# The last of a unit's seven softmax additions as an accumulating DMA from GpSimd

## The chip, the cores and the metric

The kernel runs on one core of a Trainium2 chip. The time is device microseconds of one execution. A core has five engines with queues of their own, each worked off in order: TensorE (PE; its weight loads are shown as PEld), VectorE (DVE), ScalarE (ACT), GpSimd (POOL) and SyncE (SP), which issues DMAs. Sixteen DMA engines carry the transfers. Engines wait for each other through semaphores.

## What is computed

The input is x of shape (4, 1024, 128), in fp32. Three layers follow each other: x + 0.5 FFN(layernorm(x)), then x + attention(layernorm(x)), then x + 0.5 FFN(layernorm(x)) again. The FFN is a mixture of 8 experts with routing weights. What matters here is the attention, of 16 heads of 64 in each of the 4 batches:

```
c_q, c_kv = h @ w_down_q.T, h @ w_down_kv.T
q, k, v   = up-projections of c_q, c_kv, split in heads; q and k are rotated
scores    = q @ k.T / 8                      # (4, 16, 1024, 1024)
attn      = softmax(scores)
out       = (attn @ v) @ w_out.T + residual
```

## The kernel before

**Units.** The attention is cut into 64 units. A unit is two heads (one pair P) and 512 queries; a pair has two units, an even one and an odd one. The keys come in 8 slots of 128. The probabilities stand transposed, with the keys on the partitions: a slot gives a tile p of 128 keys x (2 heads x 512 queries), 128x1024 fp32 or 512 KB.

**A unit's work.** First the scores: `score` (L921) multiplies K and Q in parts on TensorE for each slot and head and subtracts the row maxima by a fourth matmul (L933); ACT takes the exponential into p (L937). When both heads of a slot are there, `accumulate` (L941) is called. Between the scores stand the matmuls for the maxima of later slots (`passA`, L907), which DVE reduces (L908); they run 15 slots ahead. The maxima go through DRAM into one row (`max_row`, L915). At the unit's end come the denominators of the unit before (`den`), then the value matmuls (`values`, L957: the latent keys ckn times p) and ACT's copy of them (L960).

**The sums.** The softmax denominator of a query is a sum over all keys, thus over 8 slots and 128 partitions. POOL adds tiles: at slot 1 it adds p of slots 0 and 1 into acc, at each later slot it adds that slot's p to acc (L949). Seven additions give one tile acc. `den` (L962) then sums over the partitions on TensorE: a matmul with ones against acc, in four parts of 256 columns (L969; each shows as two passes, eight in all). `direct(U)` says how many of the unit's last tiles POOL leaves out: those are multiplied by ones on TensorE as well, in the same sum. Before the change it is 1 for every third unit up to 53 (U = 2, 5, ..., 53: 18 units), 3 for the last unit and 0 for the others.

**After the sums.** ACT copies the denominators to dsb (L971), SP writes them to DRAM (d<-dsb, L975) and reads them back in another order (dT<-d, L977) one unit later. DVE takes the reciprocal (rT<-dT, L988). Output matmuls with the matrix G (L992), ACT's scaling by rT (L1008) and DVE's addition to X (L1002) finish the unit. rT stands in DVE's queue between the reductions of the maxima, after the unit's scores.

**What else runs beside it.** Each unit also prepares a piece of the rotated q and k of a later pair (`rope`: matmuls L797, DVE L810 to L816, ACT L824, POOL's subtraction `lo` L832). SP writes the results to DRAM (qs, ks, 512 KB each) and loads them as QT and KT in 16 transfers of 128 KB per pair; these loads are issued in the even units. SP also fetches C_l for the next piece. The order of all this is written out by hand in `run`, with places within a unit ("mid", "end", "side", "scale").

**Buffers.** p has 10 buffers, so slot s writes into the buffer of slot s - 10. acc has 2. SP issues all DMAs of the kernel; POOL issues none.

Of the kernel before, what the change touches and what calls it, by code (L numbers as in the profile page):

```python
# [13 lines left out]
ALU = mybir.AluOpType  # L14
# [16 lines left out]
NUNIT = NSLOT // 8  # L31
# [10 lines left out]

def direct(U):

    return 3 if U == NUNIT - 1 else 1 if U % 3 == 2 and U < 56 else 0


class Kernel:
# [892 lines left out]
    def accumulate(self, s):  # L941

        nc = self.nc
        U, c = divmod(s, 8)
        if c == 0:
            self.acc_of[U] = self.accp.tile([128, 2, 512], F32, name="acc")
        elif c < 8 - direct(U):
            acc = self.acc_of[U]
            nc.gpsimd.tensor_tensor(acc, self.p_of[s - 1] if c == 1 else acc, self.p_of[s], ALU.add)  # L949
# [12 lines left out]
    def den(self, U):  # L962

        nc = self.nc
        pd = self.psS[3]
        parts = [self.p_of[8 * U + c] for c in range(8 - direct(U), 8)] + [self.acc_of[U]]
        for k, part in enumerate(parts):
            for n in range(4):
                nc.tensor.matmul(pd[32 * n:32 * n + 32, 0:256], self.ones, part[:, n // 2, 256 * (n % 2):256 * (n % 2) + 256], start=k == 0, stop=k == len(parts) - 1)  # L969
        dsb = self.op1.tile([128, 256], F32, name="dsb")  # L970
        nc.scalar.copy(dsb, pd[:, 0:256])  # L971
        dT = self.ms.tile([128, 8], F32, name="dT")

        d1 = self.dram.tile([4, 256], F32, name=f"d1_{U % 4}")
        nc.sync.dma_start(out=d1, in_=dsb[0:128:32, :])  # L975
        g = 2 * U + 4
        self.at(g + (U == NUNIT - 1), lambda: nc.sync.dma_start(out=dT, in_=d1.rearrange("(h x) (y p) -> p (h x y)", x=2, p=128)), "mid")  # L977
        self.at(g + (2 if U == NUNIT - 1 else 1), lambda: self.outp(U, self.osb_of.pop(U), dT), "side")
# [325 lines left out]
```

## Time and profile before

| | |
|---|---|
| median of 3 runs | 1623.9 us (1623.08 to 1624.63) |
| the profiled execution | 1627.57 us, of which span 1625.8 us |
| granted TensorE clock in it | 0.994 |
| attention stage | about 225 to 1465 us of the span |
| TensorE busy | 97% of the span |
| POOL busy | 90% |
| DVE, ACT busy | 76%, 68% |
| DMA engines busy, mean | 50.5% (212.27 MB moved) |

The page gives busy times by engine, a picture of the span in 40 slices, the chain of work that ended last and the costliest groups of instructions by source line. In a group's line stand the line, the engine and operation, the tiles written and read with their shapes, the count, then the busy time in us with the mean of one in ns, and the idle time of the engine before these instructions with what ended it. The chain of work that ended last is TensorE for 83% of the span; its largest pieces are the value matmuls (L957, 28%) and the scores (L933, 20%). POOL is in it with 5%, and 3% are the denominators (L969).

Other views of the same trace are used below: the timeline of one engine in a window, the busy time by engine in several windows, a source line with those that wait for it, and the list of waits. The trace also holds every count of the semaphores, from which the landing of a DMA is read.

### The profile page before, as it was taken

How to read it: one execution, taken by the hardware profiler on the slowest of the kernel's cores; microseconds unless marked ns; L12 is line 12 of the kernel's file. 1: busy time of each engine (PE TensorE's matmuls, PEld its weight loads, DVE VectorE, ACT ScalarE, POOL GpSimd, SP SyncE). 2: the span in 40 equal slices, each digit the busy share in tenths (PEclk: the TensorE clock that was granted, in tenths of full speed). 3: DMA queues.
4: the chain of work that ended last, by engine and by line, in shares of the span. 5: the costliest groups of instructions: out<-in, count | busy, mean ns of one | idle time of the engine just before them, and what ended most of it. 6: DMA issues, size and time to landing. Idle time of an engine off the chain costs nothing.

```text
span 1625.8 us, 31310 instructions
## 1 busy us (share of the span) xinstructions
PE 1575.9 (97%) x11068; PEld 1049.8 (65%) x11068; DVE 1242.0 (76%) x2198; ACT 1109.7 (68%) x2488; POOL 1464.3 (90%) x857
## 2 busy tenths in 40 slices
PE   7998999999999999999999999999999999998998
PEld 6876766566666666666666666666665666556776
DVE  6556678788888888888888887888787866616897
ACT  4676557768777667877776777776677676665554
POOL 4668889999999999999999999999999999994676
PEclk9999999999999999999999999999999999999999
DMA  7024565555555556555555566555556542025543
GB/s 226 5 60 148 169 161 133 136 152 137 144 131 138 137 147 154 144 144 131 144 131 144 132 151 159 139 151 132 143 142 156 125 105 54 2 93 145 141 131 103
DMA packets 241149, 212.27 MB, mean 131 GB/s; under 512 B 157665, under 2 KB 170593, under 8 KB 240225
## 3 DMA queue, kind: packets, MB, share of 16 engines
q1 hardware_dynamic: 240992, 210.28, 50.1%
q8 instruction: 87, 1.43, 0.4%
q14 instruction: 70, 0.57, 0.1%
HBM read 130.39 MB, written 79.82 MB: 129 GB/s over the span
## 4 chain that ended last, share of the span: by engine, by line
PE 83%; POOL 5%; DVE 4%; ACT 3%; DMA 2%; issue 2%; SPq 1%; POOLq 0%; DVEq 0%; ACTq 0%
PE psc L957 28%; PE ps_s L933 20%; PE ps_a L907 7%; PE psx L933 4%; PE psc L933 3%; PE ps_s L463 3%; PE ps_s L969 3%; PE ps_s L543 3%; PE ps_s L797 2%; PE ps_s L992 2%; PE psx L498 2%; DVE m L908 2%; DMA dT<-d 1%; POOL X L447 1%; PE psc L434 1%
## 5 line engine op out<-in xcount | busy, mean ns | idle before, releaser
L949 POOL TENSOR_TENSOR acc<-acc,p 128x1024 f32<-128x1024 f32 x363 | 864.9, 2383 | 28.4
L908 DVE TENSOR_REDUCE m<-ps_a 128x1 f32<-128x512 f32 x1024 | 674.0, 686 | 205.9 <-PE ps_a L907 175.3
L937 ACT ACTIVATE p<-ps_s 128x512 f32<-128x512 f32 x768 | 411.5, 601 | 67.3 <-PE ps_s L933 50.9
L957 PE MATMUL psc<-p,ckn 128*64 128x512 f32 x2048 | 453.6, 595 | 0.0
L933 PE MATMUL ps_s<-QT,KT 64*128 64x512 f32 x2304 | 413.2, 394 | 0.3 <-DVE C_a L718 0.3
L907 PE MATMUL ps_a<-KT,QT 64*128 64x512 f32 x1024 | 388.0, 410 | 8.9 <-DVE m L908 7.7
L957 PEld LDWEIGHTS psc<-p,ckn 128*64 128x64 f32 x2048 | 141.3, 137 | 282.1 <-issue 282.1
L933 PEld LDWEIGHTS ps_s<-QT,KT 64*128 64x128 f32 x2304 | 279.2, 184 | 61.8 <-issue 19.7
L907 PEld LDWEIGHTS ps_a<-KT,QT 64*128 64x128 f32 x1024 | 174.2, 184 | 43.8 <-DVE m L908 17.9
L960 ACT COPY osb<-psc 128x512 f32<-128x512 f32 x64 | 37.6, 587 | 230.8 <-PE psc L957 230.8
L933 PE MATMUL ps_s<-maxr,one_row 64*128 64x512 f32 x768 | 188.9, 392 | 0.0
L949 POOL TENSOR_TENSOR acc<-p 128x1024 f32<-128x1024 f32 x64 | 153.3, 2395 | 5.3 <-ACT p L937 5.3
L832 POOL TENSOR_TENSOR eo<-eo,hi_r 128x1024 fp32r<-128x1024 f32 x55 | 132.4, 2407 | 0.0
L933 PE MATMUL psx<-QT,KT 64*128 64x512 f32 x384 | 119.1, 390 | 0.0
L933 PE MATMUL psc<-QT,KT 64*128 64x512 f32 x384 | 109.2, 390 | 0.0
L933 PEld LDWEIGHTS ps_s<-maxr,one_row 64*128 64x128 f32 x768 | 99.8, 184 | 11.9
L551 POOL TENSOR_TENSOR p<-eo,p 128x512 fp32r<-128x512 f32 x42 | 62.7, 1499 | 42.3 <-ACT p L550 33.5
L1008 ACT ACTIVATE psx<-psx,rT 128x128 f32<-128x128 f32 x248 | 85.2, 344 | 20.6 <-ACT p L937 11.2
L447 POOL TENSOR_TENSOR X<-X,dtmp 128x512 f32<-128x512 f32 x54 | 69.3, 1282 | 33.1 <-ACT dtmp L446 32.0
L1008 ACT ACTIVATE ps_s<-ps_s,rT 128x128 f32<-128x128 f32 x248 | 84.3, 340 | 6.0
L824 ACT CAST hi_r<-eo 128x512 fp32r<-128x512 f32 x128 | 73.7, 626 | 18.9 <-POOL eo L819 14.1
L937 ACT ACTIVATE p<-psc 128x512 f32<-128x512 f32 x128 | 77.4, 605 | 7.8 <-PE ps_a L907 2.8
(267 smaller groups left out, 2680.9 us busy)
## 6 DMA issues: line engine op xcount, KB each, us to landing
C_l<-cs SPq DMA_DIRECT2D x128, 256.0 KB
QT<-qs SPq DMA_DIRECT2D x256, 128.0 KB
KT<-ks SPq DMA_DIRECT2D x256, 128.0 KB
qs<-hi_r SPq DMA_DIRECT2D x32, 512.0 KB
qs<-eo SPq DMA_DIRECT2D x32, 512.0 KB
ks<-hi_r SPq DMA_DIRECT2D x32, 512.0 KB
ks<-eo SPq DMA_DIRECT2D x32, 512.0 KB
rt<-wt SPq DMA_DIRECT2D x52, 256.0 KB
```

The source lines that it names most:

```text
L447: nc.gpsimd.tensor_tensor(X[:, t:t + 4, :], X[:, t:t + 4, :], tmp, ALU.add)
L463: nc.tensor.matmul(p, w[:, a, e, :], xs[:, c, :], start=k == 0, stop=k == 2)
L551: (nc.gpsimd if m < N - 1 else nc.vector).tensor_tensor(sh[:, 1, :], hp, self.f(sh[:, 0, :]), ALU.subtract)
L824: nc.scalar.copy(w["hi"][:, k, :], w["eo"][:, k, :])
L832: nc.gpsimd.tensor_tensor(w["eo"].bitcast(F32R), w["eo"], self.f(w["hi"]), ALU.subtract)
L907: nc.tensor.matmul(self.psA[hh], self.QT[P % 3][r, 0, q0:q0 + 128], self.KT[P % 3][r, 0, kk * 512:kk * 512 + 512], start=True, stop=True)
L908: nc.vector.tensor_reduce(m[0][:, hh, qb, kk:kk + 1], self.psA[hh], AX.X, ALU.max)
L933: nc.tensor.matmul(ps, w, x, start=k == 0, stop=k == 3)
L937: nc.scalar.activation(self.p_of[s][:, hh, :], ps, AF.Exp, scale=0.125)
L949: nc.gpsimd.tensor_tensor(acc, self.p_of[s - 1] if c == 1 else acc, self.p_of[s], ALU.add)
L957: nc.tensor.matmul(self.psC[64 * hh:64 * hh + 64, :], self.ckn[b % 2][:, c, :], self.p_of[s][:, hh, :], start=c == 0, stop=c == 7)
L1008: nc.scalar.activation(po[hh][:, c], po[hh][:, c], AF.Identity, scale=rT[:, 4 * hh + i:4 * hh + i + 1])
```

## The change

Two lines. `direct` now gives 3 for the last unit and 0 for every other, so that no other unit leaves a tile to TensorE. And in `accumulate` the last slot's addition is no instruction of POOL's arithmetic any more: POOL issues a DMA that adds p of slot 7 to acc in SBUF. The other six additions stay on POOL (one line further down: L949 is L951 in the changed kernel, L957 is L959, L969 is L971; the DMA is L948).

```diff
 def direct(U):
 
-    return 3 if U == NUNIT - 1 else 1 if U % 3 == 2 and U < 56 else 0
+    return 3 if U == NUNIT - 1 else 0
...
         U, c = divmod(s, 8)
         if c == 0:
             self.acc_of[U] = self.accp.tile([128, 2, 512], F32, name="acc")
+        elif c == 7 and not direct(U):
+            nc.gpsimd.dma_start(out=self.acc_of[U], in_=self.p_of[s], accum_op=ALU.add)
         elif c < 8 - direct(U):
             acc = self.acc_of[U]
             nc.gpsimd.tensor_tensor(acc, self.p_of[s - 1] if c == 1 else acc, self.p_of[s], ALU.add)
```

In the instruction order of the changed kernel the DMA stands on POOL where the seventh addition stood, behind the sixth; it waits for ACT (the last tile p) and for POOL's own sixth addition. The denominators on TensorE wait for its landing.

## The prediction

> **What bounds the kernel now.** I read the page first, its busy times and its groups. The columns of a group are line, engine, operation, tiles, count, then busy us and the mean of one in ns, then the idle time before it.
>
> ```profile
> PE 1575.9 (97%) x11068; PEld 1049.8 (65%) x11068; DVE 1242.0 (76%) x2198; ACT 1109.7 (68%) x2488; POOL 1464.3 (90%) x857
> ...
> L949 POOL TENSOR_TENSOR acc<-acc,p 128x1024 f32<-128x1024 f32 x363 | 864.9, 2383 | 28.4
> ...
> L949 POOL TENSOR_TENSOR acc<-p 128x1024 f32<-128x1024 f32 x64 | 153.3, 2395 | 5.3 <-ACT p L937 5.3
> ```
>
> TensorE and POOL both look full, so the question is which of them the other waits for. The windows of the attention stage settle it: from 300 to 1310 us TensorE is busy for 1004.4 of 1010 us and POOL for 981.5. The view of the line of POOL's additions says who waits for them.
>
> ```profile
> who waited for it (us, times):
>   PEld ps_s L969: 2.0, 7
>   ACT p L937: 1.3, 2
> ```
>
> POOL runs back to back, yet the whole kernel waits 3.3 us for its sums. **TensorE is the bound, POOL is just fast enough.** A unit is 18.7 to 21 us on TensorE; on POOL it is seven additions at 2.45 us from start to start and one subtraction L832 of 2.41, 19.6 us, or 17.1 where the eighth tile is left out. Shorter POOL time is therefore worth nothing by itself; what counts is TensorE's time and every wait that reaches it.
>
> TensorE's denominators, in the timeline of PE (start, duration, ...): a unit whose last tile goes to TensorE, and one where it doesn't.
>
> ```profile
> 411.33 0.64 PE L969 MATMUL ps_s<-p,ones 128*32 128x256 f32 x8
> 411.79 0.61 PE L969 MATMUL ps_s<-acc,ones 128*32 128x256 f32 x8
> 412.33 1.08 PE L957 MATMUL psc<-p,ckn 128*64 128x512 f32 x4
> ```
> ```profile
> 391.99 0.64 PE L969 MATMUL ps_s<-acc,ones 128*32 128x256 f32 x8
> 392.55 0.65 PE L957 MATMUL psc<-p,ckn 128*64 128x512 f32 x2
> ```
>
> From the first denominator to the first value matmul it is 1.00 us against 0.56.
>
> The third thing to read is the DMA engines. The windows of one even unit (us, busy per engine, clock, DMA share, GB/s) and SP's timeline in it:
>
> ```profile
> 393.00:396.00 3.00, 3.00 (x16) 1.00 (x14) 2.97 (x5) 2.90 (x8) 2.92 (x2) 1.00 0.95 228
> 396.00:399.00 3.00, 3.00 (x16) 1.00 (x14) 2.32 (x4) 2.81 (x8) 2.92 (x2) 1.00 0.81 232
> 399.00:402.00 3.00, 3.00 (x24) 1.98 (x22) 1.29 (x2) 1.75 (x3) 2.84 (x3) 1.00 1.06 317
> 402.00:405.00 3.00, 3.00 (x30) 2.73 (x28) 2.71 (x5) 2.92 (x7) 2.92 (x2) 1.00 1.02 183
> 405.00:406.50 1.50, 1.50 (x16) 1.47 (x14) 1.36 (x3) 1.37 (x3) 1.50 (x1) 1.00 0.10 1
> ```
> ```profile
> 399.51 2.17 SPq L57 DMA_DIRECT2D KT<-ks  x4
> 401.73 0.42 SPq L977 DMA_DIRECT2D dT<-d  x1
> ```
>
> The mean share of 0.57 hides two halves: in every second unit, the even ones that issue the loads of QT and KT, all 16 engines are full for some 12 us, and the last transfer of that burst is dT, the denominators of an odd unit. In the odd units the engines are nearly idle at this point. What a late dT costs is seen once already, at 1147 us, in the timelines of DVE and PE:
>
> ```profile
> 1147.35 0.20 DVE L988 RECIPROCAL rT<-dT 128x8 f32<-128x8 f32 x1 [1.62 <-DMA dT<-d]
> ```
> ```profile
> 1148.17 0.50 PE L907 MATMUL ps_a<-KT,QT 64*128 64x512 f32 x1 [1.55 <-DVE m L908]
> ```
>
> DVE stands 1.62 us in front of rT, the maxima behind it are late, and TensorE stands 1.55 us. A late dT passes to TensorE nearly one to one. By the trace's landing counts dT has 6.3 to 7.8 us to spare in most even units, but only 0.0 to 3.9 us (median 1.5) in the 27 odd units from 3 to 55.
>
> **The change part by part.**
>
> 1. TensorE's extra denominators. 18 units (2, 5, ... 53) lose one set of eight passes: 18 x 0.44 = **-7.9 us**, on the path.
>
> 2. POOL's additions. 427 become 382 (63 x 6 + 4): 45 x 2.38 = 107 us off POOL, off the path, worth 0 to -3.3 (the waits above); I take 0. In their place POOL issues 63 transfers. No row shows a POOL issue. SP issues a 512 KB store of the same 128 rows (C_a) in 0.34 us; its longest issues, held up by full queues, take 3.4. POOL does a 1,024-element operation of two operands in 2.38 us where DVE's two-operand operations of that size (L810) take 1.2, so I take **1.0 us**, nearer to the SP row and about twice its 0.34 to 0.57. At 1.0 POOL needs 18.1 us a unit and is nobody's bound. The turning point is 107 / 63 = 1.7 us.
>
> 3. What stands behind the issue. It waits for ACT's p of slot 7 and for POOL's own sixth addition. The additions of a unit start about 1 us after its first probabilities, whose eight tiles come in 8.2 us, so the sixth ends some 7.7 us after the eighth tile: ACT is never late, and the own wait is in the 0.06 us between additions. Behind it on POOL stand L832 (SP's store of eo waits for that) and the next unit's additions; all come earlier if the issue is under 2.4 us.
>
> 4. The wait that is added: the denominators wait for a landing instead of an addition, and behind them on TensorE stand the unit's value matmuls, ACT's copy and all that follows. They run some 20 us after the eighth tile. Replaying POOL's queue with the rows above leaves 10 to 12 us for the landing in most units and 5 to 7 in units 2, 3, 32 to 35 and 45 to 48, where POOL has extra work. The same shape without a sum (C_a's store) lands 2.6 to 3.4 us after its issue; twice its bytes (a 1 MB store of wg or wu) in 8.3 to 10.0. I take 7 us, between them, as two reads go into a full engine. That costs 3.6 us at those three places by the replay; the stalls of step 5 give POOL time, so I take **+2**. Bounds 0 (3 us) and some +17 (10 us). The buffer of the last p is next written 30 us after its tile, which covers either.
>
> 5. The DMA engines. Each transfer gives an engine 8 rows of 4,096 B of p and 8 of acc. The trace's packets of 4,096 B take 0.16 us at the least and 0.26 in the median: 8 x 0.16 = 1.3 us if the second read is free, 16 x 0.16 = 2.5 if not, 16 x 0.26 = 4.1 at most. I take 2.5, two reads at the undisturbed packet. In odd units it falls into idle time. In even units the issue ends 2 to 6 us before dT's in most cases, inside the burst. With the engines shared evenly between the two queues from 1 us after the issue, dT comes the full 2.5 us later in 13 of the 27 units, 0 to 2.1 in the others; less each unit's spare time the excess adds up to **+18.7 us**, at 1.3 us of work to 3.9, at 4.0 to 43. The cover is those 1.5 us of spare time; where it is gone, TensorE pays the rest.
>
> The Trainium skill ("DMA: Bandwidth & Descriptors", Issuing engines are not separate DMA queues) speaks against the change here: DMAs of all issuing engines interleave on the same 16 engines, so POOL's queue is no extra road. No row here has two queues in flight; by the rule step 5 is charged, without it the sum is -5.9. "Collectives: The Full Stack" (The bandwidth ceiling) says that a summing transfer is slow by its two source reads and not by its adder, at about 31 GB/s an engine: an estimate of 2.1 us for 64 KB in place of my 2.5, and a sum near +6.
>
> Sum: -7.9 + 2 + 18.7 = **+12.8 us**. The profiled execution took 1627.57 us (span 1625.8, 1.8 around it), 3.7 over the median of the runs, 1623.9; the difference is carried to the median: 1636.7, **1637 us**. Only the first term is a row; the third depends on 0.16 or 0.26 us and one read or two.
>
> **The rivals.**
> - Faster: the transfer is light (1.3 us of work or less, or it finds gaps in a burst that is held up by memory), and dT stays within its spare time. Then -7.9 and 0 to +4: **1616 to 1620**. For it: the same shape lands within 2.6 us; packets of 0.26 us against 0.16 mean engines that wait in part. Against it: spare times of 0 to 0.8 us in 10 units. The sign turns at about 1.7 us of engine work.
> - No change: between, within 3.2 us (0.2%, about what a measurement of this kernel can tell from no change): 1621 to 1627.
> - POOL becomes the bound: an issue of more than 1.7 us, for which three lists of rows (p, acc, acc again) have to be laid out. At 2.4 us POOL has 18 additions' worth more than before, 18 x 2.4 = 44, plus the landing of 7: **1675**. For it: POOL has no idle time now. Against it: SP's 0.34.
> - The change doesn't do what it says: excluded as to the sets (85 become 67); as to the issue, it must still be on POOL.
>
> **How the numbers follow.** Forecast case (late dT, +3.2 to +35: 1627 to 1659) 0.38; light transfer 0.36; no change 0.12; POOL as the bound 0.14. So faster 0.36, same 0.12, slower 0.52. The range is 1614 to 1675; left out are an issue above 2.4 us (the 3.4 of a held-up queue would give over 1,700) and gains beyond step 1, together under 2 in 10.
>
> **What would show it.** L951 x382 and a POOL DMA group x63 near 1.0 us; L971 536 passes of denominators for 680; POOL idle for some 40 us of the stage. Step 5 is right if DVE's wait for dT grows from 14.6 us (7 times) to about 30 in some 20 odd units and TensorE's wait for the maxima grows with it; wrong if it stays under 20. Step 4 is wrong if TensorE's weight loads wait for the transfer for more than 5 us. POOL still without idle time means that the issue is over 1.7 us and the third rival holds.

## The result and the profile after

The changed kernel takes **1651.23 us** (median of 4 runs, 1645.05 to 1655.04) against 1624.27 us of the kernel before on the same chip (1623.08 to 1627.29): a ratio of 1.0156, 95% interval 1.0133 to 1.0180. It is slower by 27 us. The profiled execution took 1647.92 us (span 1646.2, granted clock 0.991), 20.4 us more of span than the one of before.

The page of the changed kernel, the lines that answer to those shown of before: busy times, the DMA queue of POOL's transfers (q0: packets, MB, share of 16 engines), the chain that ended last, and groups (count, busy us, mean ns, idle time before).

```profile
PE 1573.7 (96%) x10924; PEld 1045.4 (64%) x10924; DVE 1243.4 (76%) x2198; ACT 1109.7 (67%) x2488; POOL 1418.4 (86%) x875
...
q0 software_dynamic: 9072, 33.03, 10.8%
...
PE 61%; POOL 10%; DMA 10%; SPq 8%; DVE 5%; ACT 4%; issue 3%; POOLq 0%; DVEq 0%; ACTq 0%
PE psc L959 21%; PE ps_s L933 12%; DMA dT<-d 7%; SPq L57 7%; POOL acc L951 5%; PE ps_a L907 5%; PE ps_s L463 4%; PE ps_s L543 3%; DVE m L908 2%; PE psc L933 2%; PE ps_s L971 2%; PE psx L498 2%; PE ps_s L797 2%; PE psx L933 2%; PE ps_s L994 1%
...
L951 POOL TENSOR_TENSOR acc<-acc,p 128x1024 f32<-128x1024 f32 x318 | 756.1, 2378 | 24.9
...
L907 PE MATMUL ps_a<-KT,QT 64*128 64x512 f32 x1024 | 389.3, 412 | 31.6 <-DVE m L908 29.5
...
L951 POOL TENSOR_TENSOR acc<-p 128x1024 f32<-128x1024 f32 x64 | 157.0, 2453 | 51.1 <-ACT p L937 48.9
...
L832 POOL TENSOR_TENSOR eo<-eo,hi_r 128x1024 fp32r<-128x1024 f32 x55 | 148.6, 2702 | 0.0
```

POOL is no longer full: the first addition of a unit now waits 48.9 us for ACT's probabilities (5.3 before). Nothing came of that. TensorE's share of the chain fell from 83% to 61%; what moved in are the read of dT (7%, 1% before) and SP's queue (7%). The matmuls for the maxima (L907) stood 29.5 us for DVE, 7.7 us before. The page of the kernel before has for the chain and for this line:

```profile
PE 83%; POOL 5%; DVE 4%; ACT 3%; DMA 2%; issue 2%; SPq 1%; POOLq 0%; DVEq 0%; ACTq 0%
...
L907 PE MATMUL ps_a<-KT,QT 64*128 64x512 f32 x1024 | 388.0, 410 | 8.9 <-DVE m L908 7.7
```

That is the loss: TensorE's idle time in the attention stage, 225 to 1465 us, went from 10.4 to 32.0 us.

The list of waits between 240 and 1330 us (total us, times, longest) names the way:

```profile
POOL acc L951 <- ACT p L937: 38.2, 25, 5.6
PEld ps_a L907 <- DVE m L908: 37.9, 43, 2.9
PE ps_a L907 <- DVE m L908: 26.5, 26, 2.7
DVE rT L990 <- DMA dT<-d: 26.1, 21, 2.7
```

In the same window of the kernel before, DVE waited 3.7 us, 4 times, for dT:

```profile
DVE rT L988 <- DMA dT<-d: 3.7, 4, 1.6
```

One such place in the timelines of the changed kernel, the denominators of unit 7, whose place in the kernel before the prediction shows at 399 us. SP, POOL, DVE and PE (start us, duration, ...):

```profile
397.26 0.57 SPq L977 DMA_DIRECT2D d<-dsb  x1
...
401.74 4.20 SPq L57 DMA_DIRECT2D KT<-ks  x4
405.98 0.43 SPq L979 DMA_DIRECT2D dT<-d  x1
```
```profile
400.61 0.92 POOL L948 DMA_DIRECT2D acc<-p  x1 [0.41 <-POOL acc L951]
401.27 2.70 POOL L832 TENSOR_TENSOR eo<-eo,hi_r 128x1024 fp32r<-128x1024 f32 x1
```
```profile
411.70 0.20 DVE L990 RECIPROCAL rT<-dT 128x8 f32<-128x8 f32 x1 [2.41 <-DMA dT<-d]
```
```profile
412.52 0.79 PE L907 MATMUL ps_a<-KT,QT 64*128 64x512 f32 x1 [2.34 <-DVE m L908]
```

POOL's transfer starts at 400.61, inside the burst. The four loads of KT that stand ahead of dT in SP's queue now take 4.20 us to issue (2.17 before), so dT is issued 8.7 us after the write of the denominators instead of 6.9, and lands 5.7 us after its issue (4.9 before); DVE stands 2.41 us, TensorE 2.34. Two things became late, SP's issue and the flight.

From the trace's landing counts one can follow this chain in the 28 odd units 1 to 55: ACT's copy of the denominators, the write (d<-dsb), the read (dT<-d), its landing. The steps are counted from start to start, the last one to the landing. Spare time is the time from the landing to the moment when DVE gets to rT. Means in us, with the experiments told of below (the waits are those for dT in the stage, the engine work is the sum of the transfer's packets on one engine):

| kernel | work per transfer | copy to write | write to read | read to landing | spare | waits for dT |
|---|---|---|---|---|---|---|
| before | none | 0.90 | 7.80 | 4.78 | 1.37 | 3.7 |
| after | 2.79 | 1.43 | 8.09 | 5.85 | -0.66 | 26.1 |
| e1_none | none | 0.55 | 7.75 | 4.86 | 1.56 | 0.7 |
| e12_half_alone | 1.52 | 0.98 | 7.80 | 5.39 | 0.53 | 5.6 |
| e2_copy | 1.73 | 0.72 | 7.92 | 5.94 | 0.11 | 10.9 |
| e3_odd | 2.77, odd units | 1.53 | 7.57 | 4.78 | 0.87 | 2.4 |
| e4_even | 2.78, even units | 0.66 | 7.71 | 5.74 | 0.73 | 7.2 |
| e7_even_early | 2.73, even units | 0.56 | 8.21 | 5.98 | 0.38 | 9.1 |

### The profile page after: what moved, and what is told of

It reads as the page before. It is cut to its first block, busy times and chain, and to the rows that moved or that the text cites. A ratio compares the mean times of both kernels' runs of the same rounds, so it can differ in the third digit from the quotient of the medians.

```text
span 1646.2 us, 31202 instructions
## 1 busy us (share of the span) xinstructions
PE 1573.7 (96%) x10924; PEld 1045.4 (64%) x10924; DVE 1243.4 (76%) x2198; ACT 1109.7 (67%) x2488; POOL 1418.4 (86%) x875
## 4 chain that ended last, share of the span: by engine, by line
PE 61%; POOL 10%; DMA 10%; SPq 8%; DVE 5%; ACT 4%; issue 3%; POOLq 0%; DVEq 0%; ACTq 0%
PE psc L959 21%; PE ps_s L933 12%; DMA dT<-d 7%; SPq L57 7%; POOL acc L951 5%; PE ps_a L907 5%; PE ps_s L463 4%; PE ps_s L543 3%; DVE m L908 2%; PE psc L933 2%; PE ps_s L971 2%; PE psx L498 2%; PE ps_s L797 2%; PE psx L933 2%; PE ps_s L994 1%
## 5 line engine op out<-in xcount | busy, mean ns | idle before, releaser
L951 POOL TENSOR_TENSOR acc<-acc,p 128x1024 f32<-128x1024 f32 x318 | 756.1, 2378 | 24.9
L959 PE MATMUL psc<-p,ckn 128*64 128x512 f32 x2048 | 454.6, 596 | 0.0
L907 PE MATMUL ps_a<-KT,QT 64*128 64x512 f32 x1024 | 389.3, 412 | 31.6 <-DVE m L908 29.5
L959 PEld LDWEIGHTS psc<-p,ckn 128*64 128x64 f32 x2048 | 141.6, 137 | 283.7 <-issue 283.7
L907 PEld LDWEIGHTS ps_a<-KT,QT 64*128 64x128 f32 x1024 | 174.8, 185 | 68.1 <-DVE m L908 43.3
L951 POOL TENSOR_TENSOR acc<-p 128x1024 f32<-128x1024 f32 x64 | 157.0, 2453 | 51.1 <-ACT p L937 48.9
L832 POOL TENSOR_TENSOR eo<-eo,hi_r 128x1024 fp32r<-128x1024 f32 x55 | 148.6, 2702 | 0.0
L824 ACT CAST hi_r<-eo 128x512 fp32r<-128x512 f32 x128 | 73.8, 626 | 19.4 <-POOL eo L819 14.2
```

What stands on the lines that cost most here:

```text
L824: nc.scalar.copy(w["hi"][:, k, :], w["eo"][:, k, :])
L832: nc.gpsimd.tensor_tensor(w["eo"].bitcast(F32R), w["eo"], self.f(w["hi"]), ALU.subtract)
L907: nc.tensor.matmul(self.psA[hh], self.QT[P % 3][r, 0, q0:q0 + 128], self.KT[P % 3][r, 0, kk * 512:kk * 512 + 512], start=True, stop=True)
L959: nc.tensor.matmul(self.psC[64 * hh:64 * hh + 64, :], self.ckn[b % 2][:, c, :], self.p_of[s][:, hh, :], start=c == 0, stop=c == 7)
```

## The experiments

The theory: the transfer's work on the 16 engines makes dT late in the odd units' chain, and TensorE pays what goes beyond the spare time. The rivals are named with each run. Medians are of 4 to 10 runs; the kernel before ran at 1624.5 to 1625.6 us beside them. The edits are shown against the changed kernel where no other is named.

**e1_none: no transfer.**

```diff
-            nc.gpsimd.dma_start(out=self.acc_of[U], in_=self.p_of[s], accum_op=ALU.add)
+            pass
```

> The changed kernel without the transfer: slot 7 of each unit but the last is left out of the softmax sums altogether. Theory (the transfers crowd the DMA engines, so that dT lands late): with no transfer the 18 denominator sets are a pure gain, 1613 to 1619 us, and DVE's wait for dT in the attention stage falls from 26.1 us to 4 or less. Rival (the loss lies in the changed order or in POOL's lead, not in the transfers): 1630 us or more.

Measured: 1615.45 us, ratio 0.9941 [0.9926, 0.9955]. DVE's list of waits in the stage, and TensorE's matmuls for the maxima on the page:

```profile
DVE rT L990 <- DMA dT<-d: 0.7, 2, 0.5
```
```profile
L907 PE MATMUL ps_a<-KT,QT 64*128 64x512 f32 x1024 | 388.3, 411 | 6.1 <-DVE m L908 4.8
```

The sets gone and the additions gone, without the transfer, are worth 9 to 10 us: the 7.9 of the denominators and the kernel's own waits for dT. The loss of the change, 36 us counted from here, is the transfer's, with its issue on POOL and TensorE's wait for its landing.

**e2_copy: a transfer that does not add.** It goes from p into a tile that nobody reads.

```diff
-            nc.gpsimd.dma_start(out=self.acc_of[U], in_=self.p_of[s], accum_op=ALU.add)
+            nc.gpsimd.dma_start(out=self.op1.tile([128, 2, 512], F32, name="ptmp"), in_=self.p_of[s])
```

> The transfer is issued at the same place from POOL, but as a plain copy of the last tile p into a tile that nobody reads; slot 7 is left out of the sums. One read instead of two. Theory (engine work of the transfer is what delays dT, and the second read is half of it): 8 packets of 0.16 to 0.2 us an engine instead of 0.35, DVE's wait for dT in the stage 8 to 14 us instead of 26, 1622 to 1632 us. Rival A (POOL's issue or what it does to the queue is the price, the engine work is not): the wait stays at 26, 1640 to 1655 us. Rival B (TensorE's wait for the landing is the price): 1613 to 1619 us, as no denominator waits for a copy.

Measured: 1633.65 us, 1.0051 [1.0032, 1.0071]; the waits for dT 10.9 us, 14 times. The packets of 4,096 B took 166 ns in the median (mean 216, so 1.73 us an engine and transfer), half of the accumulating ones' 332. The waits fell where the theory had them, the time is 2 us above its range. Less engine work, less loss. Rival A falls with the wait, which did not stay at 26 us. Rival B falls with the time: no denominator waits for this copy, and it still costs 18 us over e1_none. So neither the sum by itself nor the wait for the landing is the cause.

**e3_odd and e4_even: the transfer in every second unit.** Where a unit has none, every third keeps its tile on TensorE as before (nine sets) and POOL does all seven additions in the others.

```diff
-    return 3 if U == NUNIT - 1 else 0
+    return 3 if U == NUNIT - 1 else 1 if U % 6 == 2 and U < 56 else 0
...
-        elif c == 7 and not direct(U):
+        elif c == 7 and U % 2 == 1 and not direct(U):
```

(e3_odd; e4_even has `U % 6 == 5` and `U % 2 == 0`.)

> Accumulating transfers in the 31 odd units before the last only; of the even units, those that left their last tile to TensorE before (9 of them) do so again, the others add seven tiles on POOL. Theory (only the transfers inside the even units' load burst hurt): no new wait for dT, 9 sets fewer on TensorE (4.0 us), 1617 to 1624 us. Rival (every transfer has a price of its own, (27 + 7.9) / 63 = 0.55 us each): 31 x 0.55 - 4 = +13, some 1637 us.

> The mirror image: accumulating transfers in the 32 even units only, 9 of the odd units leave their last tile to TensorE, the others add seven tiles on POOL. Theory: the whole loss is in these, DVE's wait for dT some 25 us or more, 1643 to 1656 us. Rival (a price for every transfer): 32 x 0.55 - 4 = +14, some 1638 us, the same as the mirror image.

Measured: e3_odd 1621.53 us, 0.9976 [0.9966, 0.9987], waits for dT 2.4 us. It is 4.0 us faster than before, the nine sets removed: in the units whose engines stand nearly idle at that point the transfer costs nothing. e4_even 1635.79 us, 1.0070 [1.0046, 1.0094], waits 7.2 us. The place decides, as the theory says. But the theory expected 1643 us at the least for e4_even, and that is wrong. The rival's number, 1638, is nearer, yet its reason (each transfer costs the same) is refuted by e3_odd, 14 us faster with 31 transfers instead of 32. So the odd units' transfers are free alone, the even ones' cost less than half of the loss alone, and both together cost all of it.

**e7_even_early: is it the start?** In e4_even POOL has more to do, and its transfers start later against dT. Here the odd units all leave their tile to TensorE.

```diff
-    return 3 if U == NUNIT - 1 else 0
+    return 3 if U == NUNIT - 1 else U % 2
...
-        elif c == 7 and not direct(U):
+        elif c == 7 and U % 2 == 0 and not direct(U):
```

> The accumulating transfer in the even units alone, as in e4_even, but every odd unit (not only each third pair's) leaves its last tile to TensorE, so that POOL has six additions in every unit but the last and its queue runs as far ahead as in the changed kernel. TensorE has 32 extra sets of denominators instead of 18 (+6.2 us against before). Theory: e4_even was cheap because POOL ran later there and its transfers started behind dT's issue in many units; with the early start the waits for dT in the attention stage come back to 20-28 us (7.2 in e4_even) and the time is 1624 + 6.2 + 20 to 30 = 1650-1660 us. Rival: the place of the start doesn't matter and a transfer in an even unit costs what it cost in e4_even (1635.8 - 1625.6 + the 4 us of nine sets = 14): waits near 7 us, 1642-1646 us.

Measured: 1636.87 us, 1.0073 [1.0055, 1.0092], waits 9.1 us. Both fail by the time: the start explains little. The table of the chain tells what does. With transfers in the even units alone, write to landing is as late as in the changed kernel (14.2 us against 13.9), but the write itself comes 0.56 us after ACT's copy, not 1.43. e3_odd, which has transfers in the odd units only, shows that delay too (1.53). And DVE comes to rT 0.43 us later, about the 0.44 us of the set of denominators more in each odd unit. The spare time is 0.38 us instead of -0.66, the difference the sum of these. **The two halves add up in one chain, and the price begins where its spare time ends**: 0.4 us of delay by the odd transfers (e3_odd, 13.88 us from copy to landing for 13.47) fits into 1.37 in the mean and is free, 1.3 us by the even ones nearly fits, and the 1.9 of both together (0.2 more than their sum) doesn't.

The traces show where SP loses time ahead of the write. Before it in SP's queue stand a 512 KB store of eo and eight loads. In every kernel of the table the store's issue starts within 0.12 us of the later of two things, SP's instruction before it and POOL's subtraction L832. Where SP had waited 2 us or more for POOL, the issue took 0.35 to 1.36 us in the kernel before (16 units) and 0.35 to 1.23 in e4_even (10). In e3_odd, with a transfer whose issue on POOL ended 2.5 us ahead of it, it took 3.23 to 3.55 us in five of seven units, and with half the bytes (e12_half_alone below) at most 2.06. So an odd unit's transfer lengthens that issue. POOL's lateness puts the write off too, without any transfer: 0.90 us in the kernel before, whose store waits for POOL in 22 of the 28 units, and 0.55 in e1_none, where it does in one. How the 1.53 us of e3_odd divide between the two is not shown.

**e5_dtfirst and e6_before_dtfirst: dT ahead of the loads.** The same edit on the changed kernel and on the one before.

```diff
-        self.at(g + (U == NUNIT - 1), lambda: nc.sync.dma_start(out=dT, in_=d1.rearrange("(h x) (y p) -> p (h x y)", x=2, p=128)), "mid")
+        self.later.setdefault((g + (U == NUNIT - 1), "mid"), []).insert(0, lambda: nc.sync.dma_start(out=dT, in_=d1.rearrange("(h x) (y p) -> p (h x y)", x=2, p=128)))
```

> The changed kernel with one edit: dT's read is issued ahead of the four loads of KT of its place instead of behind them; nothing is added or taken out. Theory: the loss lies in dT, the last transfer of an even unit's burst. In front of the loads of KT it gains the some 2 us of SP's four issues and most of the queue, more than the 2.7 us that the transfer takes from an engine, so the waits for dT in the attention stage fall from 26.1 us to under 8 and the time to 1616-1624 us (1651 less 26 to 31). Rival: the engines are slowed for all their transfers, and the loss comes through other loads and the stores too: the waits for dT fall but the time stays at 1638 us or more.

> The same edit on the kernel before. Theory: it can give back no more than the waits for dT that the kernel before has, 3.7 us in the attention stage: 1620-1625 us. If it gains 10 us or more, dT is late for the kernel before as well, in a way that its list of waits doesn't show, and the gain of e5_dtfirst says little of the transfer.

Measured: e5_dtfirst 1626.57 us, 1.0009 [0.9999, 1.0020]; e6_before_dtfirst 1622.32 us, 0.9987 [0.9977, 0.9996]. Moving one 4 KB read within SP's queue gives back 25 of the 27 us, with every transfer still there; on the kernel before it gives 2. So most of the loss did go through dT. Not all of it: counted from e1_none the transfer's price is 36 us, and e5_dtfirst still lies 11 us above e1_none. The range was missed by 2.6 us, and DVE's list of waits in e5_dtfirst shows why:

```profile
DVE eo L815 <- DMA qs<-eo: 11.8, 9, 2.8
DVE eo L815 <- DMA ks<-eo: 10.1, 9, 1.8
...
DVE rT L990 <- DMA dT<-d: 6.2, 6, 2.1
```

Once dT is early, the next transfers to be late are the stores of eo (0.8 us in the changed kernel, none before), as the rival had it, at a fraction of its price.

**e8_odd_dtfirst: the two that helped, together** (e3_odd with the edit of e5_dtfirst).

> e3_odd (the transfer in odd units alone) with dT's read ahead of the loads of KT. Theory: it takes away the waits for dT that are left, 2.4 us in the attention stage and some in the last units: 1617-1621 us, below both kernels. Rival: dT in front makes the loads of KT late, for which TensorE waits: 1622 us or more.

Measured: 1619.25 us, 0.9973 [0.9964, 0.9983]; waits for dT 0.4 us. It is below both kernels, and no better than e3_odd within the intervals.

**e10_odd_all and e11_odd_few: how much POOL can carry.** e8_odd_dtfirst with none, and with four, of the nine sets left on TensorE.

```diff
-    return 3 if U == NUNIT - 1 else 1 if U % 6 == 2 and U < 56 else 0
+    return 3 if U == NUNIT - 1 else 0
```

(e11_odd_few: `1 if U % 12 == 8 and U < 56 else 0`.)

> e8_odd_dtfirst without the nine sets of denominators that the even units (2, 8, ... 50) still leave to TensorE: POOL adds all seven tiles of an even unit and six of an odd one, the odd one's last goes by DMA. Theory: TensorE loses another 9 x 0.44 = 4 us; POOL needs 13 x 2.45 + 1.3 + 2 x 2.4 to 2.7 = 38 to 38.5 us for a pair of units, TensorE some 38.7, so POOL just keeps up: 1615-1619 us. Rival: POOL becomes the bound, its sums come late to the denominators: 1622 us or more, with TensorE's weight loads waiting for acc by 5 us and more.

> e10_odd_all with four sets left to TensorE (units 8, 20, 32, 44), which gives POOL 10 us back over the stage. Expected between e8_odd_dtfirst and e10_odd_all if POOL keeps up in both (1616-1620 us); the best of the three if POOL is the bound in e10_odd_all (1616-1619).

Measured: 1633.28 us, 1.0050 [1.0034, 1.0065], and 1624.61 us, 1.0001 [0.9990, 1.0012]. The rival held: POOL is the bound. In e10_odd_all TensorE stands 15.0 us at the denominators, most of it for transfers that are issued late; their line's list of those who wait (us, times):

```profile
  PE ps_s L971: 10.2, 3
```

e11_odd_few expected a gain in either case and has none. The 38.0 to 38.5 us of POOL for 38.7 of TensorE was too thin a margin, POOL's other work between included; the sets on TensorE were cheap at 0.44 us each. e8_odd_dtfirst stays the fastest of the kernels that leave nothing out of the sums.

**e9_half and e12_half_alone: half the bytes.** e9_half lets POOL add one head's half and the DMA the other.

```diff
-            nc.gpsimd.dma_start(out=self.acc_of[U], in_=self.p_of[s], accum_op=ALU.add)
+            acc = self.acc_of[U]
+            nc.gpsimd.tensor_tensor(acc[:, 0, :], acc[:, 0, :], self.p_of[s][:, 0, :], ALU.add)
+            nc.gpsimd.dma_start(out=acc[:, 1, :], in_=self.p_of[s][:, 1, :], accum_op=ALU.add)
```

> The changed kernel with half the transfer: at slot 7 POOL adds the first head's half itself (512 elements a partition) and issues the accumulating DMA for the other half alone, in every unit. As many transfers and issues, half the bytes. Theory (the engine work of the transfer makes the chain of the odd units' denominators late, and it costs only what goes beyond that chain's spare time, 1.4 us in the mean): the lateness of dT's landing after the denominators were copied goes from +1.9 us to about +1, the waits for dT in the attention stage from 26.1 us to 6-12 (e2_copy with +1.1 had 10.9), the time to 1628-1636 us, so less than half the loss is left. Rival: a fixed price for each transfer (the issue on POOL, the entry in the queues) makes the loss: 1645 us or more.

Measured: 1652.31 us, 1.0171 [1.0151, 1.0190]: the rival's number. The waits of e9_half tell another story than the rival's:

```profile
PEld ps_s L973 <- DMA acc<-p: 15.9, 10, 3.7
...
PE ps_s L973 <- DMA acc<-p: 11.2, 9, 3.2
...
DVE rT L992 <- DMA dT<-d: 6.3, 9, 1.5
```

The wait for dT fell from 26.1 to 6.3 us, as the theory had it. In its place TensorE waits for the sums, because POOL is late (1492.9 us busy, 90%). The half addition takes 1.29 us and the issue 0.89, together nearly the 2.38 of the addition that they replace, and this in all 63 units, where the kernel before spared POOL 18 of its additions. The run did not separate the two theories, so the last one takes POOL's half addition away:

```diff
-            nc.gpsimd.dma_start(out=self.acc_of[U], in_=self.p_of[s], accum_op=ALU.add)
+            nc.gpsimd.dma_start(out=self.acc_of[U][:, 1, :], in_=self.p_of[s][:, 1, :], accum_op=ALU.add)
```

> The half transfer of e9_half without POOL's half addition in front of it, so that POOL keeps the early start that it has in the changed kernel. Left out of the computation: the first head's half of slot 7 in the sums of every unit but the last. In e9_half the wait for dT fell to 6.3 us as the theory had it, but POOL (1.29 us of half addition, 0.9 of issue and 0.4 in front of it, more than the 2.4 saved) became the bound and TensorE waited for the sums instead. Theory (engine work and the spare time of dT's chain): 8 x 0.19 = 1.5 us of work an engine and transfer, a little below the 1.7 of e2_copy: waits for dT in the attention stage 6-11 us, 1626-1634 us. Rival: the price is by the transfer and not by its bytes: 1645 us or more with waits for dT near 26 us.

Measured: 1621.2 us, 0.9980 [0.9970, 0.9989]; waits for dT:

```profile
DVE rT L990 <- DMA dT<-d: 5.6, 8, 1.4
```

The price goes by the bytes and not by the transfer: as many transfers with half the bytes cost 6 us over e1_none, where whole ones cost 36. The theory's range was too high by 5 us. The price is not proportional either: 0, 1.52, 1.73 and 2.79 us of engine work give waits of 0.7, 5.6, 10.9 and 26.1 us, little at first and then steep, as a spare time would make it. The four kernels differ in POOL's part as well (the copy's issue takes 0.58 us, the others' 0.9), so this is no clean curve.

**What is left over.** e2_copy lies 18 us above e1_none, and e4_even 14 us above what nine sets fewer would give (10.2 and 4.0). The waits for dT in the stage are too small for that. The pages of the profiled executions account for it in three parts. For e2_copy TensorE's idle time over the whole span is 9.6 us longer than in e1_none and its busy time 4.2; the other 4 us lie between the profiled executions and the medians. For e4_even the idle time is 6.3 us longer than before, the busy time 2.9 us more than the sets would leave, and 5.0 lie between executions and medians. The busy time may be the clock: 0.991 against 0.993 in the first pair, 0.992 against 0.994 in the second, which would be 3 to 4 us each (an estimate; a thousandth of the clock is 1.6 us of TensorE).

The clock is also part of the main result. The four executions of the changed kernel had 0.991 in the mean, the 64 of the kernel before beside the experiments 0.995: an estimate of some 6 of the 27 us. The only other kernel with 0.991 in the mean is e9_half, the one whose TensorE stands next longest in the stage (27.9 us; 32.0 in the changed kernel). Whether the standing lowers the clock is not shown; no run separates it.

## Why the prediction was right, and where its sizes were off

The direction, the place and the way were as predicted: slower, through dT in the odd units, DVE's rT, and the matmuls for the maxima one to one. The size was 12.8 us in the sum and 27 in the medians (20.4 by span between the two profiled executions). The stated range, 1614 to 1675 us, holds a gain of 10 us as well as a loss of 50, and slower had only 0.52 of the chances; so the place of the loss tells more for the prediction than the time does.

1. *TensorE's extra denominators, -7.9.* Right: e3_odd gives back 4.0 us for nine sets, e1_none 9 to 10 for eighteen and the waits for dT. In the profiles it is hidden: TensorE's busy time fell by 2.2 us only (1575.9 to 1573.7), at a clock of 0.991 for 0.994, which is worth 4.7 us.
2. *The issue at 1.0 us, POOL nobody's bound.* Right: 907 ns in the mean, and 0.4 us of idle time in front of each (25.4 us in all). The idle time is the wait for POOL's own sixth addition, which was said to be 0.06 us: in e9_half, where the instruction ahead writes the other half of acc, it isn't there. Together 1.3 us, below the turning point of 1.7. The third rival (POOL as the bound) was not met here, but it was near: e9_half and e10_odd_all run into it.
3. *What stands behind the issue.* Right in its effect. L832 looks 0.3 us longer (2702 ns for 2407), but it starts 0.26 us before the issue's end in the record, so only the border between the two moved.
4. *The denominators wait for the landing, +2.* Too high: the view of the transfer's line has the wait at 1.0 us, and the landing at 5.4 us in the median for the 7 taken.

```profile
L948 POOL DMA_DIRECT2D acc<-p x63: 876/897/1085, 241.6 to 1467.9; - x63
...
  PE ps_s L971: 1.0, 2
...
DMA to landing us min/median/max: 4.6/5.4/10.2
```

5. *The DMA engines, +18.7.* **This term was sized too small**, though not by as much as the totals suggest. The engine work was taken as 2.5 us (two reads at 0.16); measured are 8 x 0.349 = 2.79. The wait for dT was to grow from 14.6 us (7 times) to about 30 over the whole span; it grew to 42.0, 25 times, and TensorE's wait at L907 by 21.8 us (7.7 to 29.5). What the step did not see: it let the transfer delay dT's flight alone, and in the even units alone. The runs show that SP's issues ahead of dT are held up too (4.20 us for four loads for 2.17), and that the odd units' transfers, which were to fall "into idle time", go with a write of the denominators that comes 0.5 us later in the same chain (1.43 us after the copy for 0.90; 1.53 in e3_odd), in part by a longer issue of the store ahead of it. They are free only as long as the even ones leave spare time. The spare time itself was right (1.5 us in the median).

From 12.8 to 27: TensorE's idle time over the whole span grew by 22.6 us where steps 4 and 5 had 20.7, the lower clock of the profiled execution is 4.7 (an estimate), and 6.6 us lie between the executions and the medians: the profiled execution of before lay 3.3 us above its median and that of after 3.3 below. The rest, about 1 us, is unaccounted for. Step 5 itself missed by some 3 us (18.7 to 21.8); that step 4 was too high by 1 hides a part of it in the sum.

*The light transfer (0.36 of the chances).* It was put at 1.3 us of work or less, with the sign turning at 1.7. e12_half_alone with 1.52 is faster than before (1621.2) and e2_copy with 1.73 slower (1633.65), so the turning point lies where it was put, and only the transfer was heavier.

The Trainium skill's rule that DMAs of all issuing engines interleave on the same 16 engines ("DMA: Bandwidth & Descriptors", Issuing engines are not separate DMA queues) is borne out: beside POOL's transfer SP's four loads took 4.20 us to issue for 2.17. The rule that a summing transfer is slow by its two source reads ("Collectives: The Full Stack", The bandwidth ceiling) agrees with 332 ns a packet with the sum and 166 without it; no run separates the second read from the adder. The estimate from the page's 31 GB/s, 2.1 us, lies below the 2.79 measured.

## What to carry to other kernels

Before work is moved to the DMA engines, look in which stretches they are full and what is issued last in those bursts; a 4 KB transfer at the end of a burst may be the one on which a bound engine waits, and its spare time is the budget. A saving that is free in one kind of unit can cost in the other, so make the change where the engines are idle (e3_odd: 4 us faster; everywhere: 27 us slower), and before giving the work up, move the small late transfer ahead of the large ones (25 us here). Delays of different places add up in one chain: each alone may be free and both together not.

## What the runs showed of the hardware

- A packet of 4,096 B within SBUF took 332 ns with the accumulating operation and 166 ns as a plain copy, both from POOL's queue, against 156 ns at the least and 235 in the median for packets of that size in SP's queue in the changed kernel. Half the row (2,048 B) with the sum took 182 to 185 ns. (All medians but that least.)
- An accumulating DMA of 128 rows keeps POOL 0.9 us whether a row has 4,096 B (897 ns in the median) or 2,048 B (889 in e9_half); the plain copy 0.58. It lands after 4.6 to 10.2 us with whole rows and after 3.3 to 7.9 with half (e9_half 3.3 to 5.6, e12_half_alone 3.3 to 7.9).
- When another queue's transfer runs in a full stretch, SP's issues lengthen: the longest issue of dT's 4 KB read went from 602 to 1492 ns (623 in e3_odd, whose transfers lie outside those stretches). A 512 KB store that had waited 2 us or more for POOL took 0.35 to 1.36 us to issue before, and 3.23 to 3.55 in five of seven such units of e3_odd.
- POOL's addition of 512 elements a partition takes 1.29 us, of 1,024 2.38.
